# A two-layer graph network on one core: isolated rows corrected ahead, a norm shift and a reordering on GpSimd, and the last block's values later

## The chip, the cores and the metric

The kernel runs on one core of one Trainium2 chip. The metric is the device time of one launch in microseconds (us); the time before is the median of three runs. A profile comes from one further execution, whose own time is given beside its span.

The engines are named as in the profile: PE is TensorE (PEld its weight loads), DVE is VectorE, ACT is ScalarE, POOL is GpSimd and SP is SyncE, which here only issues DMAs. Each engine works through its own queue of instructions in order.

## The reference

`x` is 8 batches of 2048 nodes with 256 features, `adj` is one 2048 x 2048 matrix of zeros and ones for all batches. Layer 0 is attention over chunks of 256 keys, layer 1 is a graph attention over all 2048 keys; each works on a normed and rectified copy and is added to its input.

```python
h = maximum(layernorm(x), 0)                       # layer 0, for each of 8 batches
q, k, v = heads(h @ Wq.T + bq), heads(h @ Wk.T + bk), heads(h @ Wv.T + bv)   # 4 heads of 64
scores = clip(q . k / 8, -10, 10), and -10 where adj == 0     # [head, node, 8 chunks, 256 keys]
ctx = sum over chunks of softmax(scores, within the chunk) @ v
o = ctx @ Wo.T + bo + h
x = x + layernorm(o) * gamma + beta

h = maximum(layernorm(x), 0) @ W                   # layer 1
e = leaky_relu(h @ a1 [:, None] + h @ a2 [None, :], 0.01), and -1e9 where adj == 0
x = x + relu(softmax(e, over all 2048 keys) @ h)
```

A row of `adj` with no one in it (an isolated row) has equal weights in layer 1's softmax, so its result is the relu of the mean of `h` over all nodes.

## The kernel before

The 2048 nodes are four blocks of 512 queries (`nb`), a block being four tiles of 128 nodes (`TB` = 4). The whole program is one order written out by hand: the code runs on the host, every call appends to the queue of its engine, and nothing is reordered afterwards. Tiles come from pools with a fixed number of buffers; an instruction that writes a buffer waits until the last readers of its former content are done. PSUM has three tags, each with two buffers: `s` (two banks each, `ps_s`), `n` (`ps_n`) and `t` (`ps_t`). `ps_m` hands out `n` and `t` in turn outside the attention.

**Setup** (once). The weights are turned, batch 0 is normed and projected, and the adjacency becomes bounds in int8. It is read in 32 parts (16 tiles of 128 rows, in two halves of 1024 keys), 24 of them in setup and 8 beside the first attention steps. For a part, `load_rows` fetches int32 rows, `missing_of` (L264) writes 1 where there is no edge, as bf16, and counts those through the accumulator into `missing`; it also reorders the keys of each group of 128, reading at a step of four elements. `turn_missing` transposes the part on PE into a `t` or `n` bank and `keep_bounds` (L285) turns it into bounds on ACT. Parts of blocks 2 and 3 are then sent to DRAM, in setup by DMAs that POOL issues (L296). `find(...)` does `missing_of` for two parts and loads the rows of two later ones, `bound(...)` does the turning and keeping. `find_lone` sets `lone` to 1 for isolated rows.

**Layer 0's attention** (`Attention`). 32 steps for a batch (4 blocks, 8 chunks), each a pipeline: logits into `ps_s` (L480), clip against the bounds on DVE (L520), exponential on ACT (L529), sums over head halves on POOL (L535), values and sums on PE (L496, L508), scaling on DVE (L550), gathering by an adding DMA from POOL (L555). Between the steps stand the pieces of `Between`, which finish layer 0 for the blocks done (output weight, norm, residual) and prepare layer 1, and those that norm the next batch.

**The passage.** After the attention of a batch (`ahead` is the next batch's `Projection`), a list of calls (lines 1188 to 1251) finishes the last block, projects the next batch to q, k and v (`ahead.qk`, `ahead.values`), and makes layer 1's features. For a block, `sum1` sums the fetched features `hT` on ACT, and `ends(1)` makes four tiles of values: a product on PE (L804), a copy to `g` on ACT (L812) and a copy of the two scores to `sd` on DVE (L813). `total` and `mean` make `average`, the relu of the mean row. `targets` makes `cd` from `sd` with two exponentials, `sources(nb)` makes `src` of block 0 by transposes on PE and one exponential; later blocks get theirs through DRAM (`send`, `receive`, `received`).

**Layer 1's products.** `pieces1` are 16 pieces for a batch: 4 blocks by 4 groups of four key tiles. `weights(i)` makes the piece's weights on DVE: four times `max(src * cd0, cd1)` (L930, 128x512) and twice a masking by the bounds (L936, 128x1024), into one of five buffers of the tag `e`. `products` are 16 matmuls against `g`, two passes each (L953). The loop (L1306) makes the weights two pieces ahead. A block's four accumulators are two `ps_s` buffers for blocks 0 and 2 and the four `ps_n` and `ps_t` buffers for blocks 1 and 3. `finish(nb)` stands after the first piece of the next block. For each of four tiles it takes the sum's reciprocal on DVE (L963, L964), scales and rectifies on ACT into `r` (L966, two buffers), adds `average * lone` on DVE (L967), and adds the result to the residual tile `x4`, on POOL (L971), or on DVE for the very last block. The finish of block 3 is left to the first step of the next batch's attention (`unfinished`).

In the same loop, `far` is the projection of batch b+2: its block is loaded, and in the pieces 1, 4, 7 and 10 its `stats` are taken on DVE, `power` on ACT (three small operations) and `shift` on DVE (L344, 128x4), with `norm` on ACT and `flip` on DVE one piece later. There is a `far` for batches 0 to 5. From piece 12 on `att.early(...)` issues the first logits of the next batch's attention, into `ps_s`.

Of the kernel before, what the change touches and what calls it, by code (L numbers as in the profile page):

```python
# [9 lines left out]
BF16 = mybir.dt.bfloat16  # L10
# [3 lines left out]
ALU = mybir.AluOpType  # L14
# [3 lines left out]
P = 128  # L18
# [10 lines left out]
def gnn_two_layers(  # L29
# [18 lines left out]
    nc = tc.nc  # L48
# [3 lines left out]
    Q = P // 4  # L52
    NP = HEADS // 2
    NT = N // P
    NB = 512
    TB = NB // P
# [196 lines left out]
    HALF = N // 2  # L253
    in_setup = [True]
# [3 lines left out]
    def load_rows(t, half):  # L258
# [2 lines left out]
        nc.sync.dma_start(rows, of_block.rearrange("(p t) k -> p t k", t=TB)[:, t % TB, :])  # L261
        return rows

    def missing_of(rows, t, half):  # L264

        tag = "e" if in_setup[0] else "hn"
        z = work.tile([P, HALF], BF16, tag=tag, name="z", bufs=5)
        nc.vector.tensor_scalar(
            z.rearrange("p (k t b) -> p k t b", t=TB, b=Q), rows.rearrange("p (k b t) -> p k t b", t=TB, b=Q),
            0.0, 0.0, op0=ALU.is_equal, op1=ALU.add, accum_out=missing[:, t, half:half + 1],  # L270
        )
        return z

    def turn_missing(z):
        tag = "t"
# [593 lines left out]
    class Layer1:  # L869
# [56 lines left out]
        def weights(self, nb, j4):  # L926
            w = work.tile([P, 4, NB], F32, tag="e", name="w", bufs=5)
            for i in range(4):
                j = 4 * j4 + i
                nc.vector.tensor_scalar(  # L930
                    w[:, i, :], self.src[nb], self.cd[:, 0, j:j + 1], self.cd[:, 1, j:j + 1],
                    op0=ALU.mult, op1=ALU.max,
                )
                if i % 2:
                    two = w[:, i - 1:i + 1, :]
                    nc.vector.scalar_tensor_tensor(  # L936
                        two, bounds1[nb][:, j - 1:j + 1, :], 0.0, two, op0=ALU.is_gt, op1=ALU.mult
                    )
            return w
# [6 lines left out]
        def products(self, accs, w, j4):  # L946
# [4 lines left out]
            for i, t in pairs:  # L951
# [3 lines left out]
                    start=j == 0, stop=j == NT - 1,  # L955
                )

        def finish(self, nb, accs, store=False):
            x4 = self.blocks[nb].x4
            for t in range(TB):  # L960
                acc = accs[t]
                rz = small.tile([P, 1], F32, tag="rz1", name="rz1")
                nc.vector.tensor_scalar(rz, acc[:, F:F + 1], 1e-37, None, op0=ALU.max)  # L963
                nc.vector.reciprocal(rz, rz)  # L964
                r = work.tile([P, F], F32, tag="r", name="r")
                nc.scalar.activation(r, acc[:, 0:F], AF.Relu, scale=rz)  # L966
                nc.vector.scalar_tensor_tensor(  # L967
                    r, self.average, lone[:, nb * TB + t:nb * TB + t + 1], r, op0=ALU.mult, op1=ALU.add
                )
                adder = nc.vector if store else nc.gpsimd  # L970
                adder.tensor_tensor(x4[:, t, :], x4[:, t, :], r, op=ALU.add)  # L971
                if store:
                    rows = out[self.b, nb * NB:(nb + 1) * NB, :].rearrange("(p t) f -> p t f", t=TB)
                    nc.sync.dma_start(rows[:, t, :], x4[:, t, :])
# [128 lines left out]
    for b in range(B):  # L1103
# [84 lines left out]
        if ahead:  # L1188
            for t in range(TB):
                mid.stats1([t])  # L1190
                low.values(t)
                low.keep(t)
            zero.fetch1()
            mid.power1()
            mid.shift1()
            mid.norm1(0)
            mid.norm1(1)
            ahead.values(0)
            ahead.fetch(2)
            last.output(0)  # L1200
            last.output(1)
            mid.flip1(0, "both")
            last.take(0)
            mid.flip1(1)
            last.take(1)
            mid.send1()
            zero.sum1()
            last.stats(range(TB))
            ahead.qk(1, 0)
            last.power()  # L1210
            last.shift()
            last.scaled(range(TB))
            ahead.qk(1, 1)
            for t2 in range(2):
                last.gamma(t2)
                last.add(t2)
            for t in range(TB):
                last.stats1([t])
                zero.values(t)
                zero.keep(t)  # L1220
            mid.fetch1()
            last.power1()
            last.shift1()
            last.norm1(0)
            last.norm1(1)
            ahead.values(1)
            ahead.qk(2, 0)
            last.flip1(0, "both")
            last.flip1(1)
            last.send1()  # L1230
            ahead.fetch(3)
            mid.sum1()
            ahead.qk(2, 1)
            mid.ends(1)
            last.fetch1()
            one.send(1)
            one.send(2)
            ahead.values(2)
            one.receive(1)
            ahead.qk(3, 0)  # L1240
            last.sum1()
            last.ends(1)
            one.total()
            one.targets()
            one.sources(0)
            ahead.qk(3, 1)
            weights(0)
            one.mean()
            weights(1)
            one.send(3)  # L1250
            ahead.values(3)
        else:
            for t in range(TB):
                zero.values(t)
                zero.keep(t)
                mid.stats1([t])
            one.targets(0, TB)
            one.sources(0)
            mid.power1()
            mid.shift1()  # L1260
            low.ends(1)
            weights(0)
            mid.norm1(0)
            mid.norm1(1)
            one.targets(TB, 2 * TB)
            last.output(0)
            last.output(1)
            weights(1)
            last.take(0)
            last.take(1)  # L1270
            mid.ends(0)
            mid.ends(1)
            last.stats(range(TB))
            last.power()
            last.shift()
            last.scaled(range(TB))
            one.targets(2 * TB, 3 * TB)
            one.send(1)
            one.receive(1)
            accs[0] = one.accumulators(0)  # L1280
            early(0)
            for t2 in range(2):
                last.gamma(t2)
                last.add(t2)
            last.stats1(range(TB))
            last.power1()
            last.shift1()
            weights(2)
            last.norm1(0)
            last.norm1(1)  # L1290
            early(1)
            last.ends(0)
            last.ends(1)
            early(2)
            one.total()
            one.targets(3 * TB, NT)
            weights(3)
            one.mean()
            one.received(1)
            one.send(2)  # L1300
            one.send(3)
            one.receive(2)
            weights(4)

        far = projs[b + 2] = Projection(b + 2) if b + 2 < B else None
        for i, (nb, j4) in enumerate(pieces1):  # L1306
            if not ahead and i < 3:
                continue
            if i + 2 < len(pieces1):
                weights(i + 2)  # L1310
            if nb not in accs:
                accs[nb] = one.accumulators(nb)
            if j4 == 1 and nb + 1 < NNB:
                one.received(nb + 1)
                if nb + 2 < NNB:
                    one.receive(nb + 2)
            one.products(accs[nb], ws.pop(i), j4)
            if j4 == 0 and nb > 0:
                one.finish(nb - 1, accs[nb - 1])
            if j4 == 0 and nb > 0 and nb + 1 < NNB:  # L1320
                fetch(bounds1, nb + 1)
            if ahead and (nb, j4) == (NNB - 1, 0):
                fetch(bounds, 0)
            if j4 == 1 and nb > 0:
                one.store(nb - 1)
            if far and i in (3, 6, 9, 12):
                far.send(i // 3 - 1)
            if far and i in (0, 3, 6, 9):
                far.load(i // 3)
            if far and i in (1, 4, 7, 10):  # L1330
                far.stats(i // 3, range(TB))
                far.power(i // 3)
                far.shift(i // 3)
            if far and i in (2, 5, 8, 11):
                for t2 in range(2):
                    far.norm(i // 3, t2)
                for t2 in range(2):
                    far.flip(i // 3, t2)
            if ahead and i == len(pieces1) - 4:
                att = Attention(ahead)  # L1340
            if ahead and i >= len(pieces1) - 4 and i < len(pieces1) - 1:
                att.early(i - (len(pieces1) - 4))
                if i == len(pieces1) - 2:
                    att.early(3)
# [34 lines left out]
```

## Time and profile before

| | |
|---|---|
| runs shown | 3602.50, 3607.66, 3615.15 us (median 3607.66) |
| profiled execution | 3596.18 us, span 3594.4 us, mean granted clock 0.995 |
| PE busy | 3541.5 us, 99% of the span |
| DVE busy | 2657.2 us, 74% |
| ACT busy | 1944.8 us, 54% |
| POOL busy | 1791.0 us, 50% |
| DMA | 329.73 MB in packets, 92 GB/s on average |

How to read the views. A line of the groups or of the timeline names the start (timeline only), the busy time, the engine, the line of the code, the operation, the tile written and the tiles read, and how many; in brackets stands the idle time of the engine just before and what ended it. A line of the waits has the waiting engine and line, whom it waited for, and us in total, times and the longest. In a table of windows each row has the stretch, its length, then the busy time and the number of instructions of PE, PEld, DVE, ACT and POOL, the granted TensorE clock, the busy share of the DMA engines and GB/s. The ends of matmuls are modelled, so a PE that is 99% busy may still lose time; lengths of equal work are the safer measure.

### The profile page before, as it was taken

To read this page: it belongs to the slowest core of one execution; us is meant where nothing else is said; L and a number is where in the kernel's file an instruction comes from. 1 tells how busy PE (TensorE), PEld (TensorE's weight loads), DVE (VectorE), ACT (ScalarE), POOL (GpSimd) and SP (SyncE) were. 2 spreads that over 40 slices of the span, in tenths; PEclk is the share of its full clock that TensorE was granted. 3 is DMA by queue.
4 is the path that set the end of the run, shared out by engine and by line. 5 is a ranking of instruction groups with operands and counts; after the bars stand their busy time and mean duration, and the time that the engine had idled before them with its cause. 6 is when DMAs were issued, how large, how long until landed. Compare 5 with 4: busy or idle time off the path is not lost.

```text
span 3594.4 us, 104391 instructions
## 1 busy us (share of the span) xinstructions
PE 3541.5 (99%) x46080; PEld 2195.0 (61%) x46080; DVE 2657.2 (74%) x4007; ACT 1944.8 (54%) x2947; POOL 1791.0 (50%) x1146
## 2 busy tenths in 40 slices
PE   8999999999999999999999999999999999999999
PEld 4454775557755577555775557655586555865568
DVE  8987667876678766786677866678676785757866
ACT  6777326763267732676326762367623676147750
POOL 1687016870178702786027860278503784048831
PEclk9999999999999999999999999999999999999999
DMA  6545323443234432334323443234432334114331
GB/s 231 120 105 135 82 74 84 90 112 82 77 82 92 119 79 78 80 84 123 72 78 84 94 110 91 66 84 96 112 81 73 83 90 118 62 50 93 80 76 45
DMA packets 169110, 329.73 MB, mean 92 GB/s; under 512 B 35664, under 2 KB 97360, under 8 KB 160464
## 3 DMA queue, kind: packets, MB, share of 16 engines
q1 hardware_dynamic: 127696, 203.51, 18.3%
q0 software_dynamic: 32640, 118.50, 17.8%
q8 instruction: 360, 5.90, 0.7%
q10 hardware_dynamic: 8320, 1.05, 0.2%
q14 instruction: 94, 0.77, 0.1%
HBM read 154.14 MB, written 51.43 MB: 57 GB/s over the span
## 4 chain that ended last, share of the span: by engine, by line
PE 78%; DVE 16%; ACT 3%; issue 2%; DMA 2%; POOL 0%; ACTq 0%; DVEq 0%; SPq 0%; POOLq 0%
PE ps_s L480 24%; PE ps_n L496 24%; PE ps_t L508 6%; DVE w L936 5%; DVE w L930 5%; PE ps_n L953 3%; PE ps_t L953 3%; PE ps_s L953 3%; PE ps_t L704 2%; PE ps_t L804 2%; PE ps_s L424 2%; PE ps_n L424 2%; PE ps_t L424 2%; PE ps_n L804 2%; DVE stats L333 1%
## 5 line engine op out<-in xcount | busy, mean ns | idle before, releaser
L520 DVE SCALAR_TENSOR_TENSOR e<-ps_s,bound 128x1024 f32<-128x1024 f32 x1024 | 1225.0, 1221 | 393.5 <-PE ps_s L480 391.4
L535 POOL TENSOR_TENSOR both<-e 128x1024 f32<-128x1024 f32 x512 | 1218.2, 2404 | 544.6 <-PE ps_t L508 357.3
L480 PE MATMUL ps_s<-q,k 64*32 64x512 f32 x16384 | 1442.7, 591 | 18.4 <-ACT r L966 16.9
L529 ACT ACTIVATE e<-e 128x1024 f32<-128x1024 f32 x1024 | 1050.0, 1050 | 461.2 <-DVE e L520 443.0
L496 PE MATMUL ps_n<-e,v 64*32 64x512 f32 x16384 | 1223.3, 590 | 2.7 <-DVE prod L550 2.6
L496 PEld LDWEIGHTS ps_n<-e,v 64*32 64x32 f32 x16384 | 465.2, 107 | 468.6 <-issue 388.7
L480 PEld LDWEIGHTS ps_s<-q,k 64*32 64x32 f32 x16384 | 460.7, 106 | 468.9 <-issue 328.0
L971 POOL TENSOR_TENSOR x<-x,r 128x256 f32<-128x256 f32 x124 | 92.8, 748 | 1104.7 <-DVE rz L963 998.1
L508 PE MATMUL ps_t<-both,ones 64*32 64x512 f32 x4096 | 536.3, 591 | 0.1
L953 PE MATMUL ps_s<-g,w 128*128 128x257 f32 x2048 | 447.3, 380 | 0.0
L953 PEld LDWEIGHTS ps_s<-g,w 128*128 128x128 f32 x2048 | 388.4, 190 | 56.0
L550 DVE TENSOR_TENSOR prod<-ps_n,rz 128x512 f32<-128x512 f32 x448 | 288.9, 687 | 151.8 <-PE ps_n L496 95.4
L936 DVE SCALAR_TENSOR_TENSOR w<-bound,w 128x1024 f32<-128x1024 int8 x256 | 313.7, 1225 | 8.7
L953 PE MATMUL ps_n<-g,w 128*128 128x257 f32 x1024 | 297.9, 388 | 0.0
L953 PE MATMUL ps_t<-g,w 128*128 128x257 f32 x1024 | 294.3, 384 | 0.0
L540 ACT ACTIVATE rz<-ps_t 128x512 f32<-128x512 f32 x256 | 152.7, 596 | 228.8 <-PE ps_t L508 202.7
L930 DVE TENSOR_SCALAR w<-src,cd 128x512 f32<-128x512 f32 x512 | 259.5, 549 | 10.7 <-ACT src L911 10.3
L953 PEld LDWEIGHTS ps_n<-g,w 128*128 128x128 f32 x1024 | 196.1, 193 | 48.6 <-issue 20.7
L555 POOL DMA_DIRECT2D ctxT<-prod x224 | 190.8, 852 | 53.0 <-DVE prod L550 45.4
L953 PEld LDWEIGHTS ps_t<-g,w 128*128 128x128 f32 x1024 | 197.0, 192 | 29.7
L541 ACT ACTIVATE rz<-rz 128x512 f32<-128x512 f32 x256 | 161.4, 630 | 8.1
L966 ACT ACTIVATE r<-ps_s,rz 128x256 f32<-128x256 f32 x64 | 30.4, 475 | 246.8 <-DVE rz L964 246.8
(132 smaller groups left out, 2887.8 us busy)
## 6 DMA issues: line engine op xcount, KB each, us to landing
ctxT<-prod POOLq DMA_DIRECT2D x224, 512.0 KB, 4.8
bound<-bound_d SPq DMA_DIRECT2D x62, 1024.0 KB, 5.8
turned_d<-squares SPq DMA_DIRECT2D x232, 128.0 KB, 2.4
hT<-turned_d SPq DMA_DIRECT2D x58, 512.0 KB, 4.1
rows<-in_adj_dram SPq DMA_DIRECT2D x32, 512.0 KB, 4.9
x<-in_x_dram SPq DMA_DIRECT2D x32, 512.0 KB, 4.9
out_dram<-x SPq DMA_DIRECT2D x31, 512.0 KB, 2.7
xp<-in_x_dram SPq DMA_DIRECT2D x28, 512.0 KB, 4.5
```

The source lines that it names most:

```text
L424: nc.tensor.matmul(in_key_order(pp) if i == 0 else pp, w[:, di, do * P:(do + 1) * P], h, start=di == 0, stop=di == FC - 1,)
L480: nc.tensor.matmul(self.s[n, o][c * Q:(c + 1) * Q, kt, :], self.k[p][rows, at:at + Q], self.q[p][rows, nb * NB:(nb + 1) * NB], start=True, ...
L496: made.append(nc.tensor.matmul(self.num[n, c][h * Q:(h + 1) * Q, :], self.v[rows, j * KT + kt, at:at + Q], self.e[n, p][rows, i * KT + kt, :],
L508: nc.tensor.matmul(self.total[n][h * Q:(h + 1) * Q, :], ones[rows, :], self.both[n, h // 2][rows, h % 2, :], start=half == 1, stop=half == 0,)
L520: nc.vector.scalar_tensor_tensor(self.e[n, p][:, i * KT:(i + 1) * KT, :], self.s.pop((n, o)), -CLIP * SC, bounds[nb][:, j * KT:(j + 1) * K ...
L529: nc.scalar.activation(e, e, AF.Exp, scale=1.0 / SC)
L535: nc.gpsimd.tensor_tensor(self.both[n, p], e[:, 0], e[:, 1], op=ALU.add)
L550: nc.vector.tensor_tensor(dst[:, c, :], self.num.pop((n, c)), self.rz[n], op=ALU.mult)
L555: nc.gpsimd.dma_start(self.ctxT[nb], self.prod.pop(n), accum_op=ALU.add)
L930: nc.vector.tensor_scalar(w[:, i, :], self.src[nb], self.cd[:, 0, j:j + 1], self.cd[:, 1, j:j + 1], op0=ALU.mult, op1=ALU.max,)
L936: nc.vector.scalar_tensor_tensor(two, bounds1[nb][:, j - 1:j + 1, :], 0.0, two, op0=ALU.is_gt, op1=ALU.mult)
L953: nc.tensor.matmul(accs[t][:, 0:F + 1], w[:, i, t * P:(t + 1) * P], g[:, j, :], start=j == 0, stop=j == NT - 1,)
```

## The change

Four things change.

1. **The correction of isolated rows.** `finish` no longer adds `average * lone` to `r`. A new method `alone(nb)` adds it to the residual tile `x4` itself, in place, with the same operation and size, and is called before the third piece of each block's products. In the last batch the loop skips the pieces 0 to 2, so that the call for its block 0 is not reached.
2. **The shift of far's norm** goes from DVE to POOL (`far.adder = nc.gpsimd`).
3. **The finds in setup.** `z` has two halves there. For the second half of each row tile (12 of the 24 parts in setup) DVE now reads and writes plainly, into the second half of `z`, and a copy on POOL puts the keys in order into the first half, which PE then turns. The other 12 parts, and the 8 after setup, are done as before.
4. **The passage.** The last block's values (`last.sum1`, `last.ends(1)`) come later: ahead of them now stand `targets` for the first 12 key tiles, `sources(0)`, `weights(0)` and the keys' projection `ahead.qk(3, 1)`. `targets` for the last four key tiles follow them.

```diff
--- before.py
+++ after.py
@@ -261,15 +261,25 @@
         nc.sync.dma_start(rows, of_block.rearrange("(p t) k -> p t k", t=TB)[:, t % TB, :])
         return rows
 
+    def in_blocks(keys):
+        return keys.rearrange("p (k b t) -> p k t b", t=TB, b=Q)
+
     def missing_of(rows, t, half):
 
         tag = "e" if in_setup[0] else "hn"
-        z = work.tile([P, HALF], BF16, tag=tag, name="z", bufs=5)
+        z = work.tile([P, 2 if in_setup[0] else 1, HALF], BF16, tag=tag, name="z", bufs=5)
+        aside = in_setup[0] and half
+        apart = dict(t=TB, b=Q)
+        if aside:
+            src, dst = rows, z[:, 1, :]
+        else:
+            src, dst = in_blocks(rows), z[:, 0, :].rearrange("p (k t b) -> p k t b", **apart)
         nc.vector.tensor_scalar(
-            z.rearrange("p (k t b) -> p k t b", t=TB, b=Q), rows.rearrange("p (k b t) -> p k t b", t=TB, b=Q),
-            0.0, 0.0, op0=ALU.is_equal, op1=ALU.add, accum_out=missing[:, t, half:half + 1],
+            dst, src, 0.0, 0.0, op0=ALU.is_equal, op1=ALU.add, accum_out=missing[:, t, half:half + 1],
         )
-        return z
+        if aside:
+            nc.gpsimd.tensor_copy(z[:, 0, :].rearrange("p (k t b) -> p k t b", **apart), in_blocks(z[:, 1, :]))
+        return z[:, 0, :]
 
     def turn_missing(z):
         tag = "t"
@@ -955,6 +965,14 @@
                     start=j == 0, stop=j == NT - 1,
                 )
 
+        def alone(self, nb):
+            x4 = self.blocks[nb].x4
+            for t in range(TB):
+                nc.vector.scalar_tensor_tensor(
+                    x4[:, t, :], self.average, lone[:, nb * TB + t:nb * TB + t + 1], x4[:, t, :],
+                    op0=ALU.mult, op1=ALU.add,
+                )
+
         def finish(self, nb, accs, store=False):
             x4 = self.blocks[nb].x4
             for t in range(TB):
@@ -964,9 +982,6 @@
                 nc.vector.reciprocal(rz, rz)
                 r = work.tile([P, F], F32, tag="r", name="r")
                 nc.scalar.activation(r, acc[:, 0:F], AF.Relu, scale=rz)
-                nc.vector.scalar_tensor_tensor(
-                    r, self.average, lone[:, nb * TB + t:nb * TB + t + 1], r, op0=ALU.mult, op1=ALU.add
-                )
                 adder = nc.vector if store else nc.gpsimd
                 adder.tensor_tensor(x4[:, t, :], x4[:, t, :], r, op=ALU.add)
                 if store:
@@ -1237,16 +1252,17 @@
             one.send(2)
             ahead.values(2)
             one.receive(1)
+            one.targets(0, 3 * TB)
+            one.sources(0)
             ahead.qk(3, 0)
+            weights(0)
+            ahead.qk(3, 1)
             last.sum1()
             last.ends(1)
             one.total()
-            one.targets()
-            one.sources(0)
-            ahead.qk(3, 1)
-            weights(0)
+            one.targets(3 * TB, NT)
+            weights(1)
             one.mean()
-            weights(1)
             one.send(3)
             ahead.values(3)
         else:
@@ -1303,6 +1319,8 @@
             weights(4)
 
         far = projs[b + 2] = Projection(b + 2) if b + 2 < B else None
+        if far:
+            far.adder = nc.gpsimd
         for i, (nb, j4) in enumerate(pieces1):
             if not ahead and i < 3:
                 continue
@@ -1314,6 +1332,8 @@
                 one.received(nb + 1)
                 if nb + 2 < NNB:
                     one.receive(nb + 2)
+            if j4 == 2:
+                one.alone(nb)
             one.products(accs[nb], ws.pop(i), j4)
             if j4 == 0 and nb > 0:
                 one.finish(nb - 1, accs[nb - 1])
```

Compared queue by queue, PE has the same instructions, in another order in the passage alone; SP's issues are the same in the same order; POOL gains 12 copies and 24 shifts.

## The prediction

> **What bounds it.** I read the busy shares and the chain of waits on the page, then the length of each batch's stages from the start times of the matmuls, then the waits, and last the timeline where a stage is longer than its twin.
>
> ```profile
> PE 3541.5 (99%) x46080; PEld 2195.0 (61%) x46080; DVE 2657.2 (74%) x4007; ACT 1944.8 (54%) x2947; POOL 1791.0 (50%) x1146
> ...
> PE 78%; DVE 16%; ACT 3%; issue 2%; DMA 2%; POOL 0%; ACTq 0%; DVEq 0%; SPq 0%; POOLq 0%
> ```
>
> TensorE holds the chain, and VectorE 16% of it, nearly all in layer 1 (L936 and L930, 5% each). "Busy 99%" has modelled ends, so I compare equal work. The windows below are the products of layer 1 of batch 2, the same of batch 6, and then the passage from layer 0 to layer 1 of batches 5 and 3:
>
> ```profile
> 1301.25:1425.79 124.54, 121.73 (x593) 99.94 (x591) 94.40 (x184) 24.55 (x50) 15.08 (x16) 0.97 0.23 73
> 3073.32:3190.62 117.30, 117.30 (x593) 98.05 (x591) 82.30 (x140) 14.03 (x23) 15.55 (x16) 1.00 0.13 45
> 2575.90:2629.97 54.07, 53.72 (x204) 37.60 (x201) 26.87 (x71) 28.55 (x71) 4.59 (x4) 1.00 0.43 87
> 1690.60:1750.74 60.14, 55.57 (x204) 38.70 (x201) 26.88 (x71) 29.13 (x70) 4.60 (x4) 0.97 0.42 79
> ```
>
> The same 593 matmul records take 124.5 us in batch 2 and 117.3 in batch 6, at a clock of 0.97 and 1.00. From first to last product, batches 0 to 6 take 124.34, 124.33, 124.32, 121.00, 121.01, 124.31 and 117.08 us: 36.8 us above batch 6's pace in all. The passages take 54.34, 55.09, 54.33, 60.47, 56.38, 54.34 and 54.33: 9.0 us above 54.33. Setup (before 85 us) has some 9 us of gaps. These are what a change off TensorE's own work can win.
>
> Where the products lose it (batch 3, finish of block 2):
>
> ```profile
> 1839.97 0.15 DVE L963 TENSOR_SCALAR rz<-ps_s 128x1 f32<-128x1 f32 x1
> ...
> 1841.79 0.47 ACT L966 ACTIVATE r<-ps_s,rz 128x256 f32<-128x256 f32 x1 [0.88 <-DVE rz L964]
> 1842.30 0.48 DVE L967 SCALAR_TENSOR_TENSOR r<-mean,lone,r 128x256 f32<-128x256 f32 x1 [0.60 <-ACT r L966]
> ...
> 1842.32 1.06 PE L480 MATMUL ps_s<-q,k 64*32 64x512 f32 x8 [1.15 <-ACT r L966]
> ...
> 1844.52 0.47 ACT L966 ACTIVATE r<-ps_s,rz 128x256 f32<-128x256 f32 x1 [0.88 <-DVE rz L964]
> 1845.05 1.92 PE L480 MATMUL ps_s<-q,k 64*32 64x512 f32 x24 [1.67 <-ACT r L966]
> ```
>
> The next batch's first logits need the two banks of `ps_s` that `finish(2)` empties. The accumulators were complete by about 1834, but VectorE, late with its weights, began finish only at 1839.97 and then spent 1.3 us per tile, half of it waiting for ScalarE's `r`. TensorE idles 1.15 + 1.67 us. In batches 0, 1, 2 and 5 the trace's clock records then show half clock for 6.83 us, worth 3.4 us more: the two sizes of loss, 3.9 and 7.2. Batch 6, which has no batch b+2 to prepare, has no stall.
>
> ```profile
> DVE r L967 <- ACT r L966: 78.5, 128, 0.6
> DVE krn L344 <- ACT krn L340: 22.8, 28, 0.8
> ```
>
> ```profile
> PE ps_z L282 <- DVE hT L398: 3.9, 2, 1.9
> PE ps_z L282 <- DVE z L268: 3.5, 3, 1.3
> ```
>
> The first pair is what VectorE waits for in finish and far's shift over the whole run; the second is TensorE's own list for the first 95 us. The last place is the passage of batch 3, where TensorE waits for the last block's features and then runs 3.41 us at half clock:
>
> ```profile
> 1731.21 1.88 PE L424 MATMUL ps_n<-hT,wqT 128*128 128x512 f32 x4
> 1737.31 1.57 PE L804 MATMUL ps_t<-w1s,hT 128*128 128x258 f32 x4 [4.22 <-DMA hT<-turned_d]
> ```
>
> [...] The find at L268 reads int32 at a step of four[...] and takes 2069 ns for 1024 elements, where a plain 128x1024 at L520 takes 1221[...]; the trace's two-input 128x1024 at L535 takes 2404 ns[...].
>
> **Part 1, the correction.** `finish` loses 128 operations at L967 (485 ns each) and their 128 waits (0.6 us each). `alone` puts 124 on VectorE earlier, at the third piece of each block; they read `average`, `lone` and `x4`, ready long before, so they wait for nothing. (The last batch's loop skips pieces 0 to 2, so its block 0 has none.) A finish of four tiles falls on VectorE from 5.4 us to about 4 x 0.35 = 1.4. On ScalarE the four relus then run at 0.5 us apiece, or at GpSimd's 0.75 since `r` has two buffers: the last ends 3.0 us after the start, not 5.0. GpSimd's adds now wait for ScalarE directly; behind them is only the shift of part 2.
>
> **Part 2, the shift.** Four shifts of far each leave VectorE, 0.16 us and 0.84 of waiting: 4.0 us in a batch. GpSimd takes 486 ns for one, behind the four adds of finish, and its reader is the norm one piece (7 us) later: nothing on the path. Uncovered it would delay one ScalarE norm by 0.5 us.
>
> **Part 3, the passage.** sources(0) (0.44 us of TensorE) and the keys' qk(3,1) (3.43) move ahead of `last.ends(1)`; the total work is the same. They fill the wait for the features: of batch 3's gap about 0.4 us stays and its slow clock goes (5.6 of 6.1 won), batches 1 and 4 lose all of theirs (0.8 and 2.0). Sum 8.4 us. `weights(0)` needs only the first 12 columns of `cd`, so it runs in VectorE's idle time before the sd copies (0.7 to 9 us at a time); behind it wait only those copies, and it ends (about 1735.5 in batch 3's time) before they are due. SP's issues do not change order.
>
> **The stall at finish(2), summed.** From weights(0) at 1744.39 to finish(2) at 1839.97 VectorE has 95.6 us. Out: one weights tile 4.4, shifts 4.0, two finishes 2 x 4.0. In: three `alone`, 12 x 0.485 = 5.8. Net 10.6 us earlier, and about 1 us more because weights(1) needs no new `src`. TensorE starts the products 3.9 us nearer to `ends(1)`, so VectorE's lead grows by 7.7 us. Needed is 3.1 us (banks free by 1841.9 instead of 1845.0), of which finish's own shortening gives 2.0. So the stall goes in batches 0 to 5, and its slow clock with it: 36.8 us. `alone(3)` adds 1.9 us ahead of a clip whose `ps_s` has 5.8 us to spare (1857.2 against 1863.05).
>
> **Setup.** Twelve finds read plainly on VectorE; I price one at 1.22 us (L520's row), bounds 1.1 and 2.07 (the cost is the form's, not the step's). That is 10 us less for VectorE, but TensorE has only 1.9 + 1.9 of gaps there that a faster find opens at once. Against it stand GpSimd's 12 copies: the trace has no such operation[...]. The last copy stands in GpSimd's queue behind the DMA issues of parts 20 and 21, which end at 78.63, and TensorE wants it at 77.64: 2.6 us lost. Net gain 1 us, from -4 (plain reads no faster[...]) to +8 (all gaps closed).
>
> **Tail.** The last tile's chain loses one operation of 0.5 us: 0.6 with its handover.
>
> **Sum.** 36.8 + 8.4 + 1 + 0.6 = 46.8 us, against the profiled execution's 3596.18 (span 3594.4): 3549. The median shown is 3607.66, 11.5 above that execution. If that excess lies elsewhere (as in waits for gathered products), it stays: **3561 us**; if it is more of the same stalls, down to 3549.
>
> **Rivals.** (a) VectorE gets no earlier, because its lead is eaten by something that the trace of before does not show[...]. Then only finish's shape helps: the banks come 0.9 and 2.0 us sooner, about 1.5 us of loss a batch stays, no slow clock: 36.8 - 9 = 28, total 38, about 3570. For it: VectorE is never idle there[...]. (b) The stall stays whole, since the banks wait on GpSimd's adds through `r`'s two buffers: only part 3, setup and tail, 0 to 10 us: 3598 to 3608. Against: four adds are 3.0 us. (c) Slower: GpSimd's reordering of 4 dimensions is far dearer than its elementwise rows. Twelve copies in series bind setup, 68 us long from 14 to 82, once one takes over 5.7 us, and outweigh the 46.8 above 9.6 us; at 11 us, 3625. Against: 2404 ns for twice the inputs.
>
> **Numbers.** All stalls gone 0.78 (own range 3545 to 3575), (a) 0.13, (b) 0.05, (c) 0.04. What this kernel's measurement tells from no change is about 0.3%, 11 us. Faster 0.91, same 0.05, slower 0.04. Range 3541 to 3590: below it takes in the 11.5 us and a setup gain of 8; above it (a) with the poor setup.
>
> **What would show it.** Right: products of 117 us in all of batches 0 to 6, no half clock there; no wait of L480 on `r`; passages near 54.3; VectorE's waits on `r` gone; finds of about 1.2 us beside those of 2.07. Wrong: a stall of L480 of over 1 us in any batch, copies over 3 us, or z waiting on GpSimd for more than 5 us in setup.

## The result, and the profile after

The changed kernel takes 3565.11 us (median of 4 runs, 3561.53 to 3566.59) beside 3610.57 us for the kernel before on the same occasion: a ratio of 0.9875, interval 0.9854 to 0.9896, 45.5 us. The forecast was 3561 in 3541 to 3590. The profiled execution took 3563.89 us (span 3562.1, clock 0.998).

The time by stage, from the start times of the matmuls. The second profiles are further executions of the same two kernels, made among the experiments; the last column is the best kernel found there.

| us | before | before, second | after | after, second | both mends |
|---|---|---|---|---|---|
| start to the end of batch 0's attention | 359.2 | 363.1 | 358.9 | 362.0 | 356.2 |
| attentions of batches 1 to 6 | 1585.5 | 1584.0 | 1587.5 | 1583.7 | 1580.5 |
| seven passages | 389.3 | 392.8 | 389.6 | 389.1 | 380.9 |
| products of batches 0 to 6 | 856.4 | 860.0 | 819.6 | 819.6 | 819.6 |
| last batch | 404.0 | 405.7 | 406.5 | 404.8 | 405.9 |
| span | 3594.4 | 3605.6 | 3562.1 | 3559.1 | 3543.0 |

The unreached call of `alone(0)` has a consequence: an isolated row in block 0 of the last batch goes without its mean, in this kernel and in every one below that has the correction. That takes four additions off VectorE (four of them take 1.67 us elsewhere), in the last batch alone, where no gain shows.

Against the profiled execution that the forecast started from, the products gave 36.8 us, to the tenth what was reckoned. The passages gave nothing, where 8.4 had been reckoned. The page of the changed kernel, its busy times and the shares of its chain:

```profile
PE 3527.6 (99%) x46080; PEld 2183.0 (61%) x46080; DVE 2639.0 (74%) x3979; ACT 1947.4 (55%) x2961; POOL 1808.9 (51%) x1182
...
PE 97%; DVE 1%; DMA 1%; ACT 1%; issue 0%; POOL 0%; ACTq 0%; DVEq 0%; POOLq 0%; SPq 0%
```

VectorE is as busy as before (74%), but its share of the chain is 1% instead of 16%: nearly the same work, no longer late. The table of windows, for the products of batches 2 and 6 and the passages of batches 5 and 3 (the clock is the third number from the end):

```profile
1288.50:1405.70 117.20, 117.20 (x593) 98.07 (x592) 91.08 (x177) 24.38 (x50) 16.17 (x21) 1.00 0.29 81
3038.50:3155.80 117.30, 117.30 (x593) 98.06 (x592) 79.93 (x137) 13.62 (x22) 15.71 (x17) 1.00 0.13 44
2545.10:2600.60 55.50, 54.32 (x212) 37.54 (x202) 29.45 (x75) 29.81 (x73) 4.60 (x4) 1.00 0.40 83
1670.50:1726.20 55.70, 54.52 (x211) 37.46 (x202) 29.47 (x75) 29.66 (x73) 4.60 (x4) 1.00 0.41 83
```

Batch 2's products have batch 6's length and the full clock. The two passages are now alike: batch 3's 60.47 us has become 55.63, but batch 5's 54.34 has become 55.40, as have five of the seven.

The timeline at `finish(2)` of batch 3. The line numbers have moved: L963 is now L981, L966 is L984, L971 is L986, L480 is L490; of `ends(1)`, L804 is L814, L812 is L822 and L813 is L823.

```profile
1808.43 0.15 DVE L981 TENSOR_SCALAR rz<-ps_s 128x1 f32<-128x1 f32 x1
...
1809.49 3.11 POOL L986 TENSOR_TENSOR x<-x,r 128x256 f32<-128x256 f32 x4 [9.75 <-ACT r L984]
...
1811.21 0.48 ACT L984 ACTIVATE r<-ps_s,rz 128x256 f32<-128x256 f32 x1 [0.48 <-DVE rz L982]
1816.53 1.95 PE L490 MATMUL ps_s<-q,k 64*32 64x512 f32 x32
```

The last relu ends at 1811.69, and the logits start 4.8 us later, 32 in a row with no wait ahead of them. Before, the same logits went out in two pieces with idle times of 1.15 and 1.67 us. Over the whole run TensorE's waits on `r`, 16.9 us in 12 places, are gone. What TensorE waits for instead is in its list of waits (line waiting, whom for, us in total, times, longest):

```profile
PE ps_z L292 <- POOL z L281: 6.5, 4, 4.3
PE ps_n L890 <- DVE hsum L898: 5.8, 7, 0.8
```

The second of the two is the passages' loss: once in each of seven batches. The timeline of batch 3's passage shows it, first on TensorE, then on VectorE:

```profile
1719.93 1.03 PE L814 MATMUL ps_t<-w1s,hT 128*128 128x258 f32 x4
1721.79 1.10 PE L890 MATMUL ps_n<-w1s,hsum 128*128 128x256 f32 x4 [0.83 <-DVE hsum L898]
```

```profile
1719.49 0.16 DVE L823 COPY sd<-ps_n 128x2 f32<-128x2 f32 x1 [3.92 <-ACT g L822]
...
1721.42 0.16 DVE L823 COPY sd<-ps_t 128x2 f32<-128x2 f32 x1 [0.71 <-ACT g L822]
1721.49 0.15 DVE L898 TENSOR_REDUCE hsum<-sums 128x2 f32<-128x8 f32 x1
```

`mean`'s product (L890) needs `hsum`, which `total` makes on VectorE (L898). `total` stands behind the four `sd` copies of `ends(1)`, the last of which follows TensorE's last value and ScalarE's copy to `g`. In the kernel before, `sources(0)` and `qk(3, 1)` stood between the two and filled the time; the change moved both ahead of `ends(1)`.

The first wait is the last reordered part in setup. The timeline there, first GpSimd, then TensorE:

```profile
73.03 1.80 POOL L306 DMA_DIRECT2D bound_d<-bound_part  x2 [0.89 <-ACT bound_part L303]
74.83 1.09 POOL L281 COPY z<-z 128x1024 bf16<-128x1024 bf16 x1
```

```profile
75.97 1.03 PE L292 MATMUL ps_z<-ident_b,z 128*128 128x128 bf16 x8 [4.25 <-POOL z L281]
```

The copy, whose find on VectorE ended at 72.17, waits in GpSimd's queue behind two issues of DMAs, until 74.83; TensorE waits 4.25 us, and the trace then has 3.41 us of half clock from 75.4.

### The profile page after: what moved, and what is told of

Read it like the earlier page. It is cut to its first block, busy times and chain, and to the rows that moved or that the text cites. A ratio compares the mean times of both kernels' runs of the same rounds, so it can differ in the third digit from the quotient of the medians.

```text
span 3562.1 us, 104433 instructions
## 1 busy us (share of the span) xinstructions
PE 3527.6 (99%) x46080; PEld 2183.0 (61%) x46080; DVE 2639.0 (74%) x3979; ACT 1947.4 (55%) x2961; POOL 1808.9 (51%) x1182
## 4 chain that ended last, share of the span: by engine, by line
PE 97%; DVE 1%; DMA 1%; ACT 1%; issue 0%; POOL 0%; ACTq 0%; DVEq 0%; POOLq 0%; SPq 0%
PE ps_s L490 25%; PE ps_n L506 24%; PE ps_s L963 12%; PE ps_t L518 7%; PE ps_n L963 6%; PE ps_t L963 6%; PE ps_t L714 2%; PE ps_t L434 2%; PE ps_n L434 2%; PE ps_s L434 2%; PE ps_t L814 2%; PE ps_n L814 2%; PE ps_t L448 1%; PE ps_n L448 1%; DVE z L277 0%
## 5 line engine op out<-in xcount | busy, mean ns | idle before, releaser
L530 DVE SCALAR_TENSOR_TENSOR e<-ps_s,bound 128x1024 f32<-128x1024 f32 x1024 | 1224.1, 1220 | 404.0 <-PE ps_s L490 400.6
L490 PE MATMUL ps_s<-q,k 64*32 64x512 f32 x16384 | 1431.8, 590 | 1.5 <-DVE e L530 1.4
L490 PEld LDWEIGHTS ps_s<-q,k 64*32 64x32 f32 x16384 | 459.5, 106 | 448.6 <-issue 331.2
L963 PE MATMUL ps_s<-g,w 128*128 128x257 f32 x2048 | 447.8, 380 | 0.0
L963 PEld LDWEIGHTS ps_s<-g,w 128*128 128x128 f32 x2048 | 388.8, 190 | 56.3
L986 POOL TENSOR_TENSOR x<-x,r 128x256 f32<-128x256 f32 x124 | 90.7, 745 | 466.2 <-ACT r L984 465.4
L963 PE MATMUL ps_n<-g,w 128*128 128x257 f32 x1024 | 292.4, 382 | 0.0
L963 PE MATMUL ps_t<-g,w 128*128 128x257 f32 x1024 | 289.7, 380 | 0.0
L963 PEld LDWEIGHTS ps_n<-g,w 128*128 128x128 f32 x1024 | 192.8, 190 | 44.3 <-issue 17.6
L963 PEld LDWEIGHTS ps_t<-g,w 128*128 128x128 f32 x1024 | 193.8, 189 | 28.2
```

Of the source, the lines that this page charges most:

```text
L490: nc.tensor.matmul(self.s[n, o][c * Q:(c + 1) * Q, kt, :], self.k[p][rows, at:at + Q], self.q[p][rows, nb * NB:(nb + 1) * NB], start=True, ...
L530: nc.vector.scalar_tensor_tensor(self.e[n, p][:, i * KT:(i + 1) * KT, :], self.s.pop((n, o)), -CLIP * SC, bounds[nb][:, j * KT:(j + 1) * K ...
L963: nc.tensor.matmul(accs[t][:, 0:F + 1], w[:, i, t * P:(t + 1) * P], g[:, j, :], start=j == 0, stop=j == NT - 1,)
```

## The experiments

Four kernels make one part of the change alone; the kernel before ran beside them at 3607.65 us (median of 15 runs, 3597.25 to 3615.15).

**The correction alone** (`alone` instead of the addition in `finish`).

```diff
+            if j4 == 2:
+                one.alone(nb)
             one.products(accs[nb], ws.pop(i), j4)
```

> The kernel before with part 1 alone (the correction on x4 ahead of finish; as in the changed kernel, the last batch's block 0 is left uncorrected). Theory (VectorE is late at finish(2)): two finishes are 4.0 us shorter each and three corrections cost 5.8, so VectorE comes 2.2 us earlier, and the third finish is 2.0 us shorter; 4.2 us in all against 3.1 needed, so the stall of the next batch's logits goes in batches 0 to 5, with its half clock: products of 117 us in all seven batches, 36 us less in the profile. Passages stay at 54.3 plus what the features' DMAs cost. Rival (the stall needs all the parts, because VectorE is never idle there and takes back what it is given): 1 to 2 us of stall stay in each batch, products of 119 to 121, 20 us less.

Measured: 3577.81 us, ratio 0.9918 (0.9899 to 0.9937). The products are 118.96 us in batches 0 to 5, without half clock: 1.9 us of the stall stay in each. The timeline of batch 3, VectorE and then TensorE:

```profile
1825.20 0.15 DVE L971 TENSOR_SCALAR rz<-ps_s 128x1 f32<-128x1 f32 x1
...
1826.17 0.16 DVE L971 TENSOR_SCALAR rz<-ps_s 128x1 f32<-128x1 f32 x1 [0.62 <-ACT r L974]
...
1827.49 0.16 DVE L971 TENSOR_SCALAR rz<-ps_s 128x1 f32<-128x1 f32 x1 [0.71 <-ACT r L974]
```

```profile
1827.15 1.06 PE L480 MATMUL ps_s<-q,k 64*32 64x512 f32 x8 [0.53 <-ACT r L974]
1828.47 1.92 PE L480 MATMUL ps_s<-q,k 64*32 64x512 f32 x24 [0.26 <-ACT r L974]
```

VectorE reaches finish(2) only 0.2 us earlier against the products. Between weights(0) and finish(2) the timelines give: finish(0) 2.6 us instead of 5.4, since the second and fourth reciprocal still wait for a relu; finish(1) 1.1 instead of 5.6; the three `alone` put 4.8 in; and VectorE waits 2.3 us more for ScalarE's norm of `far` behind finish(1):

```profile
1800.30 0.71 DVE L136 STREAM_TRANSPOSE squares<-hn 128x512 f32<-128x512 f32 x1 [2.83 <-ACT hn L356]
```

That is 2.8 + 4.5 - 4.8 - 2.3 = 0.2. What the correction buys is the shape of finish, whose last relu ends 3.2 us after its first reciprocal instead of 5.0.

**The shift alone** (`far.adder`).

```diff
         far = projs[b + 2] = Projection(b + 2) if b + 2 < B else None
+        if far:
+            far.adder = nc.gpsimd
```

> The kernel before with part 2 alone (far's shift on GpSimd). Theory (lateness): four shifts of 0.16 us and their 0.84 us of waiting are 4.0 us before finish(2), more than the 3.1 needed, though finish keeps its shape: stall gone or under 0.5 us, products of 117 to 118 in batches 0 to 5, 30 to 36 us less. Rival (the shape of finish is what counts): the second pair of banks still comes 5 us after finish begins, the stall stays near 2.8 us with its half clock in some batches, products of 121 to 124, under 10 us less.

Measured: 3562.80 us, ratio 0.9876 (0.9857 to 0.9896), the gain of the whole change. The products are 117.08 to 117.42 us, no half clock in them. Finish is as it was, with its waits for `r`; it only begins earlier:

```profile
1813.29 0.15 DVE L963 TENSOR_SCALAR rz<-ps_s 128x1 f32<-128x1 f32 x1
...
1818.42 0.48 DVE L967 SCALAR_TENSOR_TENSOR r<-mean,lone,r 128x256 f32<-128x256 f32 x1 [0.60 <-ACT r L966]
```

```profile
1818.38 1.98 PE L480 MATMUL ps_s<-q,k 64*32 64x512 f32 x32
```

The last relu ends as the logits start: this part covers the need with nothing to spare.

**The passage alone.**

```diff
             one.receive(1)
+            one.targets(0, 3 * TB)
+            one.sources(0)
             ahead.qk(3, 0)
+            weights(0)
+            ahead.qk(3, 1)
             last.sum1()
             last.ends(1)
             one.total()
-            one.targets()
-            one.sources(0)
-            ahead.qk(3, 1)
-            weights(0)
+            one.targets(3 * TB, NT)
+            weights(1)
             one.mean()
-            weights(1)
```

> The kernel before with part 4 of the change alone (the last block's values later, weights(0) ahead of them). Theory: VectorE starts 5.4 us earlier but TensorE begins the products 3.9 us nearer to the values, so the lead is 1.5 us of the 3.1 needed: the stall shrinks from 2.8 to about 1.3 us in batches 0 to 5, half clock less often, products of 118.5 to 122. Every passage is 55.4 us, not 54.3, for the mean's product now stands right behind the last values and waits for the total on VectorE. In all 10 to 25 us less. Rival (the passage is worth its 8 us of waits): passages of 54.3 and the products as before.

Measured: 3573.78 us, ratio 0.9911 (0.9893 to 0.9929). Products 118.4 to 118.7 us in batches 0 to 5, no half clock; passages 55.40 in five batches, 56.57 and 55.90 in the others. The 1.07 us a batch come with this part and need no other.

**The finds alone** (as in the change's first hunk).

```diff
-        return z
+        if aside:
+            nc.gpsimd.tensor_copy(z[:, 0, :].rearrange("p (k t b) -> p k t b", **apart), in_blocks(z[:, 1, :]))
+        return z[:, 0, :]
```

> The kernel before with part 3 alone (12 finds read plainly, ordered by GpSimd). Theory: a plain find is 1.22 us for 2.07, a copy 1.12; TensorE gains 3 to 4 us up to part 20 and gives them back at the last copy, which stands behind two DMA issues: setup within 1 us of before, products of 124 and 121 as before, no change in the total beyond what DMAs vary. Rival (setup was VectorE's): 8 to 10 us less.

Measured: 3601.59 us, ratio 0.9987 (0.9974 to 1.0): no gain to speak of. The stall is whole (products 121.0 to 124.1 us), and two passages of 60.0 and 60.7 us appear, in batches 0 and 4.

The single gains are 30, 45, 34 and 6 us, together far more than the 45 of all four: three of the parts pay for one stall. The table shows it for batch 3, with times relative to the start of the last product ahead of the logits:

| kernel | finish(2)'s first reciprocal | its last relu ends | products |
|---|---|---|---|
| before | -0.82 | 4.20 | 121.00 |
| correction alone | -1.04 | 2.18 | 118.96 |
| passage alone | -3.46 | 1.56 | 118.4 |
| shift alone | -4.78 | 0.31 | 117.11 |
| after | -7.79 | -4.53 | 117.08 |

The earlier starts add up: 0.22 + 2.64 + 3.96 = 6.8 us, where all together give 6.97. (1.07 of the passage's 2.64 is TensorE's own wait ahead of `mean`, by which the products begin later; the run with the old passage, below, shows it.) The time they buy does not: it ends when the relu is done about 0.3 us after that product starts.

**Only the order: finish first.** The kernel before, with finish issued one weights piece earlier in the loop.

```diff
         for i, (nb, j4) in enumerate(pieces1):
...
+            if j4 == 0 and nb > 0:
+                one.finish(nb - 1, accs[nb - 1])
             if i + 2 < len(pieces1):
                 weights(i + 2)
...
             one.products(accs[nb], ws.pop(i), j4)
-            if j4 == 0 and nb > 0:
-                one.finish(nb - 1, accs[nb - 1])
```

> The kernel before, with the four instructions of each finish tile issued ahead of the weights of the piece i + 2 and of the products of the piece i, not behind them. No work is removed or moved to another engine. VectorE then comes to finish(2) one weights piece (4.4 us) earlier, about 5.2 us ahead of the products that precede the logits instead of 0.82. If lateness alone makes the stall, the last relu ends near 0.2 us before or after the logits are due, no half clock stands in the products, and all of them are 117 to 118 us: 3563 to 3570. If what counts is how finish is built (relu, addition and GpSimd's add through two buffers), the stall of some 2.8 us a batch and its half clock stay: 3600 to 3608. If VectorE, now waiting for the accumulators, makes the next weights late, TensorE waits in the products themselves: over 118 us without a wait of L480.

Measured: 3578.90 us, ratio 0.9929 (0.9910 to 0.9948); products 119.5 us. The wait at finish(2) is gone (first reciprocal at -5.20, last relu at -0.21), with no work removed: lateness alone made it. But 2.4 us come back one piece later (and two passages of 61 us, with late features, stand in this profile):

```profile
1829.14 1.95 PE L480 MATMUL ps_s<-q,k 64*32 64x512 f32 x32
...
1839.44 3.05 PE L480 MATMUL ps_s<-q,k 64*32 64x512 f32 x32 [1.22 <-DVE e L520]
```

The second logits need the banks that the clip (L520) of the first releases, and the clip now stands behind two pieces of weights. So the order moves the deadline from finish to the clip; taking work away moves both (TensorE waits on the clip for 8.6 us here, in seven places of which one is in setup; in the changed kernel for 1.4 us, in setup alone). The forecast of 117 to 118 us failed there, and it was the clip that came late, not the weights.

**The two mends.** They and the changed kernel ran together; the kernel before was at 3604.73 us beside them (9 runs, 3593.01 to 3610.74). The total ahead of the last values:

```diff
             last.sum1()
-            last.ends(1)
             one.total()
+            last.ends(1)
```

> The changed kernel, with `one.total()` moved ahead of `last.ends(1)`. Theory (the passage lost its gain because the mean's product stands right behind `ends(1)` and waits for `hsum`, which VectorE makes only after the four sd copies): the 0.83 us of idle ahead of `mean` goes and every passage of an undelayed batch is 54.3 us long instead of 55.40, so 7 x 1.07 = 7.5 us less than the changed kernel, near 3557. Products stay at 117.1 us in all batches. Rival (the passage is longer because the new order of matmuls itself costs more, as in a bank that is not free or a weight load that is not covered): passages stay at 55.4 us and the time at 3565.

The last of the reordered parts found the old way:

```diff
-        aside = in_setup[0] and half
+        aside = in_setup[0] and half and t != 11
```

> The changed kernel, with the last of the 12 reordered parts in setup found the old way, so that no copy on GpSimd stands behind the DMA issues of earlier parts. Theory: TensorE's wait of 4.25 us at 75.97 us falls to about 1 us and the half clock at 75.4 us goes (1.7 us), so setup is 4 to 5 us shorter than in the changed kernel: near 3560. Rival (the plain finds moved the bound of setup to the loads or to ScalarE's bounds, and the wait only shows it): another wait of 3 to 4 us takes its place, within 1 us of 3565.

Both:

> The changed kernel with both mends: the total ahead of the last values, and the last reordered part found the old way. If the two losses are separate places on TensorE's chain, they add up: 7.5 + 4.5 = 12 us less than the changed kernel, near 3553, passages 54.3 us and no wait of over 1.5 us on z in setup. If one of them is only cover for a transfer that comes late anyway, 4 to 8 us: 3557 to 3561.

The changed kernel again:

> The changed kernel again, as the measure for the three runs beside it, and for what differs between two profiled executions of one kernel. 3565 us (3561 to 3567); products 117.1 us in all batches, passages 55.4 us but for one or two that wait for a transfer (1 to 2 us more), 4.25 us of wait on z at 76 us, as these follow from the order of instructions. Where the half clock lies in the last batch may differ by 3.4 us.

Measured: the changed kernel 3559.55 us (0.9878, 0.9860 to 0.9897), total first 3552.81 (0.9863, 0.9845 to 0.9881), last find the old way 3556.68 (0.9870, 0.9851 to 0.9889), both 3547.47 (0.9850, 0.9830 to 0.9871). A single mend's 3 to 7 us lie within what these intervals can tell, so the stages are the better witness; both together are 12.1 us. With the total first, five passages are 54.33 or 54.34 us (54.92 and 56.38 the others) instead of 55.40. In the kernel with both mends TensorE's timeline has no wait at the mean:

```profile
1710.53 1.03 PE L814 MATMUL ps_t<-w1s,hT 128*128 128x258 f32 x4
1711.40 1.02 PE L890 MATMUL ps_n<-w1s,hsum 128*128 128x256 f32 x4
```

and in setup a shorter one:

```profile
74.55 0.62 PE L292 MATMUL ps_z<-ident_b,z 128*128 128x128 bf16 x8 [1.29 <-DVE z L277]
```

The start up to batch 0's attention is 354.4 to 358.4 us in the four profiles with the second mend, 358.9 to 362.0 in the four with the finds as in the change. The changed kernel's second profile has the same 117.08 and, but for batch 4 (56.65), 55.40 us: these lengths belong to the order of instructions, not to chance. Half clock near 76 us, for 3.41 or 6.83 us, stands in all four profiles with the finds as in the change and in none of those with the second mend.

**The kernel before, once more.**

> The kernel before, once more, for a second profile: the profiled execution shown was 11 us below the median of its runs. If the excess lies in passages that wait for the transposed features (as the passages of 59 to 61 us in batches 0, 3 and 4 of the runs with one part alone suggest), its products are again 36 +- 3 us in all above batch 6's pace, and passages of 59 to 61 us stand in other or more batches. If it lies in the stall at finish(2), the products' sum is 45 us or more above that pace.

Measured: 3607.35 us, the usual time of its runs. Against the execution shown first (table above) the 11.2 us of span lie in setup and batch 0 (3.9), the passages (3.5), the products (3.6) and the last batch (1.7), less 1.5 in the attentions. Neither reading of the expectation was right: it is a little of each, the products standing 40.4 us above batch 6's pace in all, between the 36 and the 45. The products differ by their half clock alone; the waits are the same:

```profile
PE ps_s L480 <- ACT r L966: 16.8, 12, 1.7
PE ps_t L804 <- DMA hT<-turned_d: 7.9, 4, 3.2
```

**The old passage, with the rest mended** (both mends' kernel beside it; the kernel before at 3605.36 us, 9 runs, 3599.67 to 3618.95).

```diff
-            one.targets(0, 3 * TB)
-            one.sources(0)
             ahead.qk(3, 0)
-            weights(0)
-            ahead.qk(3, 1)
             last.sum1()
-            one.total()
             last.ends(1)
-            one.targets(3 * TB, NT)
-            weights(1)
+            one.total()
+            one.targets()
+            one.sources(0)
+            ahead.qk(3, 1)
+            weights(0)
             one.mean()
+            weights(1)
```

> The kernel with both mends (total ahead of the last values, last reordered part found the old way), but with the passage in the order of the kernel before. If the order of the passage is worth what it hides of late features (0.8 to 6 us in two or three batches) once the total is made early, this one is 5 to 12 us slower than the kernel beside it: 3553 to 3560, with one to three passages of 56 to 61 us and the others at 54.33. Products 117.1 us all the same, since the shift and the correction give VectorE 4.2 us of lead. If the features come late only by chance of one execution, within 3 us of it.

> The kernel with both mends again, beside the one with the old passage and on another occasion: 3547 us (3543 to 3553), passages 54.3 us in all batches but one or two of up to 56.4, no half clock in the products and none from the wait on z in setup.

Measured: 3558.16 us with the old passage (0.9865, 0.9845 to 0.9886), 3545.14 with both mends (0.9831, 0.9813 to 0.9849). Their seven passages are 391.2 and 381.3 us in all, the products 117.08 in both. In the old order the features come late by several us in two batches (60.53 and 58.05 us), here batch 0:

```profile
400.32 2.06 PE L814 MATMUL ps_t<-w1s,hT 128*128 128x258 f32 x4 [3.10 <-DMA hT<-turned_d]
402.17 1.93 PE L814 MATMUL ps_n<-w1s,hT 128*128 128x258 f32 x4
```

The second line is at half clock, 1.93 us for what takes 1.03. In the new order batch 4 keeps 0.67 us of that wait, and no other batch any.

The lead at finish(2) of batch 3 belongs here too. The first reciprocal stands at -5.16 with the old passage and at -6.80 with both mends, so the new order gives VectorE 1.64 us, where it gave 2.64 in the passage alone. The missing 1.0 is the wait ahead of `mean`: it made TensorE late by that much, and with the total made early it is gone.

The kernel with both mends is the best version: 3545 to 3547 us, some 12 us below the change. Whether the shift with the mended passage and nothing else would do as well was not tried.

## Why the prediction was right, and where it was not

**The stall** (36.8 us reckoned, 36.8 measured): right, and by its mechanism: VectorE came late, and everything that makes it earlier helps. The lead was put at 7.7 us and is 7.0. Its terms were less well sized. The shift's 4.0 us are 3.96. The two finishes less three `alone`, 8.0 - 5.8 = 2.2, are 0.22 (2.8 + 4.5 - 4.8, less the 2.3 of waiting): the prediction saw that ScalarE's relus run at GpSimd's pace (an add took 0.75 us before and after), but not that VectorE's own next flip waits for the norm behind those relus, nor that reciprocals of accumulators in `ps_s` keep a wait. So VectorE's waits on `r`, which were to go, stay with 21.4 of 78.5 us. The passage, 5.4 - 3.9 = 1.5, is 2.64, but only 1.6 of that is VectorE's: the rest is TensorE's wait ahead of `mean`, a loss in the passage that counts as lead in the products. Without it the lead would be about 5.9. The need, put at 3.1 us, was nearer 3.9, as the shift alone shows, which has 3.96 and none left. The lead was still 2 to 3 us above the need, so the wrong sizes cost nothing. The prediction named no part as sufficient by itself; the shift is. That the figure agrees to the tenth is chance, for how much half clock the stall draws differs between executions: against the second profile of the kernel before, the same 36.8 would have stood beside 40.4.

**The passage** (the prediction's part 3, the fourth of the change; 8.4 us reckoned, -0.3 measured): the step that failed. The prediction's "They fill the wait for the features" holds: with the total made early, the new order is worth 391.2 - 381.3 = 9.9 us. What it missed is what the two pieces had been filling where they were taken from. It counted the gap ahead of `ends(1)` and not the one behind it, where `mean` waits for `total`: 55.40 - 54.33 = 1.07 us in each of seven batches, 7.5 in all. Over all profiles the seven passages take 389.3 to 394.5 us in the old order (seven profiles), 389.1 to 389.6 in the order of the change (four), and 380.9 to 383.0 with the total early (three). The profile that the forecast started from had the shortest of the old order; against it nothing of the gain was left, against the others 0 to 5 us. With the total early, 6.3 to 8.4 us of the 8.4 come.

**Setup** (+1 reckoned, +0.3 measured between the two profiles; the start up to batch 0's attention takes 359.2 to 363.1 us in the six profiles with the old finds and 358.9 to 362.0 in the four with the new, so no gain can be told). The groups of the changed kernel:

```profile
L277 DVE TENSOR_SCALAR_CACHE_REDUCE z<-rows 128x1024 bf16<-128x1024 int32 x32 | 55.3, 1779 | 0.1
L281 POOL COPY z<-z 128x1024 bf16<-128x1024 bf16 x12 | 13.4, 1118 | 52.3 <-DVE z L277 52.3
L354 POOL TENSOR_TENSOR krn<-krn,mv 128x4 f32<-128x4 f32 x28 | 6.8, 242 | 575.4 <-DVE w L940 575.4
```

The mean of 1779 ns holds 12 plain finds of 1.24 us, near the 1.22 priced, and 20 strided ones of 2.10. A copy took 1.12 us. The prediction's loss of 2.6 us at the last one counts 1.6 for it (78.63 + 1.6 - 77.64), the author's own estimate, which nothing in the trace of before showed; the +1, a balance with that loss, rests on it too. The mean of 242 ns holds four shifts in batch 0 that GpSimd did before as well (0.46 to 0.50 us); the 24 new ones took 0.20 each, less than half the 486 ns assumed. The late copy behind the DMA issues was foreseen and put at 2.6 us; it is 4.25 and a window of half clock: TensorE, served faster, was there at 71.72 instead of 77.64, while the issues ended at 74.83 instead of 78.63. The test named for "wrong", more than 5 us of waiting for GpSimd's `z`, did come true (6.5).

**The tail's** 0.6 us can't be seen: the last batch differs between two executions of one kernel by 1.7 us before, 1.7 after and 3.0 with both mends.

**The step from the profiled execution to the median.** The sum of 46.8 us met 32.3 between the two profiles, but 45.5 between the medians. The 14.5 missing lie in the passages (8.7), the last batch (3.1), the attentions (2.0) and setup (0.7). The prediction let the excess of 11.5 us of before's runs stay. The second profile of before shows that some of it belonged to what the change mends (3.6 us of half clock in the products, 3.5 of late features). So that 3561 came out 4 us from 3565 is in part luck, for two errors met: the passage's gain that did not come, and an excess that partly went. The rivals fall: VectorE did get earlier (a), TensorE never waited behind GpSimd's adds (b), though the relus did, for 5.8 us in the whole run, and a copy took 1.12 us (c). Rival (a) holds for the correction by itself, whose lead was eaten, though by the wait for `far`'s norm; four additions of `alone` take 1.67 us, less than the 1.9 reckoned.

## What to carry to other kernels

Where several parts of a change serve one deadline, add up the lead that each gives and compare it with what is needed, not their times: here one part of four, moving four tiny operations a batch, with their waits, to an idle engine, was enough. Before moving work into a gap, ask what it covers where it stands; two lines later a reduction needed by TensorE may be bare, and making that reduction early cost nothing here. And treat one profiled execution as a sample: compare stages whose lengths repeat to a hundredth (here 117.08 us for the products and 55.40 for the passages).

## What was not expected of the hardware

- Equal stalls drew unequal half clock. With idle times of 1.15 + 1.67 us, one execution of the kernel before had no half clock in batch 3, and the 24 logits after them took 1.92 us; with 1.13 + 1.67 us another had 10.24 us of it there, and they took 3.64. Over both profiles it lasted 0, 3.41, 6.83 or 10.24 us, and the products took 121.0, 122.6, 124.3 or 125.3. That stall costs 3.9 us without half clock; the smaller ones, 2.4 us with finish first, 1.9 with the correction alone and 1.3 with the passage alone, drew none in six batches each.
- A GpSimd copy of 128x1024 bf16 with reordering took 1118 ns, where the addition of two 128x1024 f32 (L535 of the kernel before) took 2404. What of it is due to the number of inputs and what to their type was not tried.
- The finds of the same 12 parts took 2.01 us at a step of four in the kernel before and 1.24 us plainly in the changed one. The pair differs in the order of the keys alone, and the code writes consecutive elements both times, so it is the reading that differs.
- One operation on GpSimd, `krn<-krn,mv` of 128x4, took 0.46 to 0.50 us in four places of batch 0 and 0.20 in 24 beside layer 1's products, in one execution (spans on GpSimd are rough). What sets them apart was not tried.
- In finish, the reciprocals on `ps_s` waited for `r` in 32 places, 21.4 us in all; those on `ps_n` and `ps_t` never did. In `ps_s` two accumulators share a buffer, in the others one has its own. Whether the sharing is the cause was not tried.
